# Row attention of the middle stage in eight slots, with TensorE in program order and the masked queries on ScalarE

## The chip, the cores and the metric

The kernel runs on one core of a Trainium2 chip. The metric is device time in microseconds, the median of several executions. Such a core has five engines that run side by side and wait for each other by semaphores: TensorE (matrix products and transposing[...]), VectorE, ScalarE, GpSimd, and SyncE, which here only issues DMAs. PSUM has eight banks per partition; this kernel uses six of them under one tag (`mm`) and two under another (`sm`).

## The reference

The input x has shape (4, 64, 256, 256). Layer 0 is a restormer-like block: layer normalisation over channels, a gated attention branch, a convolutional feed-forward branch whose result passes an 8x8 patch FFT with a learned filter, and residual additions. Layer 1 is attention along rows, then along columns, then a small MLP. The change lies in the piece that ends layer 0 and does the row attention of layer 1. Cut to that:

```python
# end of layer 0: 1x1 product, 8x8 patch FFT filter, residual
y = _conv1x1(y, out_w)
p = y.reshape(b, c, Hh // P, P, Ww // P, P).transpose(0, 1, 2, 4, 3, 5)
p = jnp.fft.irfft2(jnp.fft.rfft2(p) * fW, s=(P, P))
x = x + p.transpose(0, 1, 2, 4, 3, 5).reshape(b, c, Hh, Ww)
# layer 1, along each row; H = 4 heads, one query and one key value per head
q = jax.nn.elu(x @ wq.T + bq) + 1.0
k = jax.nn.elu(x @ wk.T + bk) + 1.0
q = q / q.mean(axis=3, keepdims=True)
k = k / k.sum(axis=3, keepdims=True)
ktv = jnp.einsum('brhcd,brhce->brhde', k, v)
o = jnp.einsum('brhcd,brhde->brhce', q, ktv)
h = xe + o.swapaxes(2, 3).reshape(b_, r_, c_, e_) @ wo.T + bo   # x is _ln(xe)
```

## The kernel before

The program runs in stages, each with its own pools: a, b and c1 (attention and input side of layer 0), c2 (depthwise convolutions as banded products), c3 (this change), d (column attention and MLP). c2 leaves its result in DRAM (`yd`), c3 leaves the hidden state in DRAM (`hd`), and d reads it.

Stage c3 works on tiles `(pr, s)`: a pair of images and a strip of eight image rows, 64 tiles in all. Per tile there are five generators, each a part of the work:

- `product` (line 962): the 1x1 product. For each of four row pairs r, two matrix products (line 970), one per image of the pair, with 512 columns; ScalarE copies the result to `zc` (line 971). Then 16 transposing products in groups of four (line 980), copied to `zs` by ScalarE (line 981).
- `patches` (line 985): for each half, the DFT of the patches (line 997), VectorE's multiplication with the filter into `fs` (line 1001), the inverse (line 1007), the residual addition into `xe` (line 1010), and the layer norm's sums (lines 1013 to 1018); at the end ScalarE's square root (line 1021) and VectorE's reciprocal into `rs`.
- `features` (line 1026): four times, `xe` is transposed (line 1033), copied to `xrT` by ScalarE (line 1035) and multiplied with the query and key weights into the `sm` bank `qk` (line 1038, "score"). Then VectorE transposes the result (line 1043), scales it and adds a bias, ScalarE takes the exponential (line 696), VectorE forms `f` (line 1050) and `kr` (line 1056). `f` is spread into masked copies for each of eight image rows: keys `kx` by eight ScalarE activations (line 1058), queries `qx` by one GpSimd multiplication (line 1059). Row sums go into `qj` and `kj` on VectorE (lines 1065, 1066).
- `attend` (line 1069): sums of keys times `xe` (line 1079), two products for the row sums (lines 1081, 1082), eight transposing products of `qx` (line 1095) with ScalarE's copies, a folding product (line 1100), and `mix` (line 699, product at line 702), which ends in `bdm` (line 1106).
- `update` (line 1109): four products of one row for the bias (line 1115), eight products of `qT` with `bdm` (line 1119), four VectorE additions into `h1` (line 1121), four DMAs issued by GpSimd (line 1125).

The loop at line 1131 runs n from 0 to 67. It first issues the loads of tile n + 1 from SyncE (`ya` and `xmp`), then gives `_steps` (line 241) five generators for five different tiles: `product` of tile n, `patches` of n - 1, `features` of n - 2, `attend` of n - 3, `update` of n - 4. `_steps` asks each in turn for its next part up to a `yield`, round after round, until all are exhausted. In 60 of the 68 loops all five are present.

The order in which the generators speak is the order of the program. It isn't yet the order on the engines: a planner places the instructions of each engine with its own model of costs and readiness, and within one engine may put a later instruction ahead of an earlier one. Stage d switches that off for TensorE:

```python
with tc.manual_schedule(engines={mybir.EngineType.PE}):
```

Inside it, TensorE's instructions stand in the order of the program, while the other engines are still placed by the planner. Stage c3 has no such line. The engines themselves take what they were given in order: an instruction that waits holds up those behind it on its engine.

Buffers that bear on this: `zc`, `fs`, `qTr`, `u`, `f`, `h1` have one buffer, `xe` and `xmp` three, most others two.

Of the kernel before, what the change touches and what calls it, by code (L numbers as in the profile page):

```python
# [9 lines left out]
F32 = mybir.dt.float32  # L10
AF = mybir.ActivationFunctionType
ALU = mybir.AluOpType
# [237 lines left out]
def kernel(ctx: ExitStack, tc: tile.TileContext, x, packs, fd, out, off):  # L250
# [670 lines left out]
    def stage_c3():  # L921
        NS = H // 8
        with ExitStack() as cs:
# [38 lines left out]
            def product(pr, s):  # L962

                ya, _ = ld[pr, s]

                zc = p.tile([128, 32, 32, 2], F32, name="zc", bufs=1)
                for r in range(4):
                    t = mm()
                    for b in (0, 1):
                        T.matmul(t[b * 64:(b + 1) * 64, :], owT, ya[:, :, 2 * r:2 * r + 2, b * 64:(b + 1) * 64].rearrange("p f y t -> p y f t"), start=True, stop=True)  # L970
                    S.copy(zc[:, :, 8 * r:8 * r + 8].rearrange("p j f t -> p f j t"), t.rearrange("p (f j t) -> p f j t", f=8, t=2))
                    if r % 2:
                        yield
                zs = p.tile([128, 16, 2 * C], F32, name="zs")
                zss[pr, s] = zs
                for k in range(4):
                    t = mm()
                    for i in range(4):
                        j = 2 * (4 * k + i)
                        T.transpose(t[:, i * 128:(i + 1) * 128], zc[:, j:j + 2].rearrange("p j f t -> p (j f t)"), ident)  # L980
                    S.copy(zs[:, 4 * k:4 * k + 4].rearrange("p g c -> p (g c)"), t)
                    if k % 2:
                        yield

            def patches(pr, s):

                _, xmp = ld.pop((pr, s))
                zs = zss.pop((pr, s))
                xe = p.tile([128, 16, 2 * C], F32, name="xe", bufs=3)
                sv = p.tile([128, 32], F32, name="sv")  # L990
                for hf in (0, 1):

                    zh = zs[:, 8 * hf:8 * hf + 8].rearrange("p (n g) c -> p n (g c)", n=2)
                    ts = [mm(), mm()]
                    for pt in (0, 1):
                        for n in (0, 1):
                            T.matmul(ts[pt][n * 64:(n + 1) * 64, :], dfw[pt * 64:(pt + 1) * 64, :], zh[pt * 64:(pt + 1) * 64, n], start=True, stop=True)
                    fs = []
                    for pt in (0, 1):
                        f_ = p.tile([128, 512], F32, tag=f"fs{pt}", name=f"fs{pt}", bufs=1)  # L1000
                        V.tensor_tensor(f_.rearrange("p (g c) -> p g c", c=C), ts[pt].rearrange("p (g c) -> p g c", c=C), mid_bc(fw, 8), ALU.mult)
                        fs.append(f_)
                    yield
                    ts = [mm(), mm()]
                    for pt in (0, 1):
                        for n in (0, 1):
                            T.matmul(ts[n][pt * 64:(pt + 1) * 64, :], dfi[n * 64:(n + 1) * 64, :], fs[pt][n * 64:(n + 1) * 64, :], start=True, stop=True)
                    for n in (0, 1):
                        r = slice(8 * hf + 4 * n, 8 * hf + 4 * n + 4)
                        V.tensor_tensor(xe[:, r].rearrange("p g c -> p (g c)"), ts[n], xmp[:, r].rearrange("p g c -> p (g c)"), ALU.add)  # L1010
                    src = xe[:, 8 * hf:8 * hf + 8].rearrange("p g (b c) -> p (g b) c", b=2)
                    s1 = p.tile([128, 16], F32, name="s1")
                    V.tensor_reduce(s1, src, AX.X, ALU.add)
                    xc = p.tile([128, 16, C], F32, name="xc")
                    V.scalar_tensor_tensor(xc, bc(s1, C), -LN_S, src, ALU.mult, ALU.add)
                    sq = p.tile([128, 16, C], F32, name="sq")
                    S.activation(sq, xc, AF.Square)
                    V.tensor_reduce(sv[:, 16 * hf:16 * hf + 16], sq, AX.X, ALU.add)
                    yield
                sd = p.tile([128, 32], F32, name="sd")  # L1020
                S.activation(sd, sv, AF.Sqrt, bias=eps_t, scale=LN_S)
                rs = p.tile([128, 32], F32, name="rs")
                V.reciprocal(rs, sd)
                xes[pr, s] = xe, rs

            def features(pr, s):

                xe, rs = xes[pr, s]
                qk = sm()
                for k in range(4):  # L1030
                    t = mm()
                    for i in range(4):
                        T.transpose(t[:, i * 128:(i + 1) * 128], xe[:, 4 * k + i], ident)
                    xT = p.tile([128, 512], F32, name="xrT")
                    S.copy(xT, t)

                    for g in range(4):
                        T.matmul(qk[g * 32:(g + 1) * 32, k * 128:(k + 1) * 128], rw, xT.rearrange("p (j n) -> p j n", j=4)[:, :, g * 32:(g + 1) * 32],
                                 start=True, stop=True)
                    yield  # L1040

                qp = p.tile([128, 16, 32], F32, name="qp")
                V.transpose(qp.rearrange("p j m -> p (j m)"), qk)
# [12 lines left out]
                V.tensor_tensor(kr, f[:, :, 4:8], bc(rs, 4), ALU.mult)  # L1056
                for y in range(8):
                    S.activation(kx[:, :, y], kr, AF.Identity, scale=rmask[:, y:y + 1])
                G.tensor_tensor(qx, f[:, :, 0:4].unsqueeze(2).to_broadcast([128, 32, 8, 4]), mk.to_broadcast([128, 32, 8, 4]), ALU.mult)
                fr = p.tile([128, 2, 8], F32, name="fr")  # L1060
                V.tensor_reduce(fr, f.rearrange("p (j b) h -> p b h j", b=2), AX.X, ALU.add)
                qj = p.tile([128, 2, 2, 8, 4], F32, name="qj")
# [6 lines left out]
            def attend(pr, s):  # L1069

                xe, _ = xes.pop((pr, s))
                qx, kx, qj, kj = fes.pop((pr, s))
                yield
                zp = sm()

                for j in range(16):
                    for b in (0, 1):
                        g = (2 * b + j % 2) * 32
                        T.matmul(zp[g:g + 32, :64], kx[:, 2 * j + b].rearrange("p y h -> p (y h)"), xe[:, j, b * 64:(b + 1) * 64], start=(j < 2), stop=(j >= 14))
                qs = mm()  # L1080
                T.matmul(qs[:, 0:1], qj.rearrange("p d b y h -> p (d b y h)"), K0("ones"), start=True, stop=True)
                T.matmul(qs[:, 1:2], kj.rearrange("p b d y h -> p (b d y h)"), K0("ones"), start=True, stop=True)
                rz = p.tile([128, 1], F32, name="rz")
                V.reciprocal(rz, qs[:, 1:2])
                qr = p.tile([128, 1], F32, name="qr_")
                V.tensor_copy(qr, qs[:, 0:1])
                zn = p.tile([128, 65], F32, name="zn")
                G.memset(zn[:, 64:65], 0.5)
                V.tensor_scalar(zn[:, 0:64], zp[:, 0:64], rz, None, ALU.mult)
                qT = p.tile([128, 1024], F32, name="qTr", bufs=1)  # L1090
                for k in (0, 1):
                    t = mm()
                    for i in range(4):
                        j = 8 * k + 2 * i
                        T.transpose(t[:, i * 128:(i + 1) * 128], qx[:, 2 * j:2 * j + 4].rearrange("p a y h -> p (a y h)"), ident)
                    S.copy(qT[:, k * 512:(k + 1) * 512], t)
                yield
                t = mm()

                T.matmul(t[:65, :64], zn, K("rfold"), start=True, stop=True)  # L1100
                zT = p.tile([65, 2, 64], F32, name="zT")
                V.tensor_copy(zT, mid_bc(t[:65, :64], 2))
                yield
                m = mix(p, zT.rearrange("p j y -> p (j y)"), rgt, qr)
                bdm = p.tile([128, 4, 64], F32, name="bdm")
                V.tensor_tensor(bdm, mid_bc(m, 4), bc(K("jmask"), 64), ALU.mult)
                bds[pr, s] = xe, qT, bdm

            def update(pr, s):

                xe, qT, bdm = bds.pop((pr, s))
                h1 = p.tile([128, 2, 16, C], F32, name="h1", bufs=1)
                ts = [mm() for k in range(4)]
# [9 lines left out]
                for b in (0, 1):  # L1123
                    for a in (0, 1):
                        G.dma_start(hd[2 * pr + b, 8 * s:8 * s + 8, 8 * a:8 * a + 8], h1[a * 64:(a + 1) * 64, b])
                yield

            seq = [(pr, s) for pr in range(B // 2) for s in range(NS)]
            load(*seq[0])

            for n in range(len(seq) + 4):
                if n + 1 < len(seq):
                    load(*seq[n + 1])
                _steps(*(f(*seq[n - d]) for d, f in ((1, patches), (4, update), (3, attend), (2, features), (0, product)) if 0 <= n - d < len(seq)))

    stage_c3()

# [275 lines left out]
```

## Time and profile before

| | us |
|---|---|
| median of 3 runs | 8800.12 (8797.13 to 8805.94) |
| the profiled execution | 8803.6 |
| its span, first to last instruction | 8801.8 |
| stage c3, first product to last update on TensorE | 5056.8 to 6675 |
| stage d, first product | 6689.7 |

The page gives TensorE 93% of the span busy, VectorE 67%, ScalarE 52%, GpSimd 14%. In its rows a shape such as `128*64 128x512` means: a tile of the array with 128 rows and 64 columns, and a moving operand of 128 partitions by 512 elements. One fp32 product of the program is two matrix instructions in the trace. "TensorE" is PE in the rows, "VectorE" DVE, "ScalarE" ACT, "GpSimd" POOL. What stands in brackets after a row of the timeline is the idle time of the engine before it, and what ended it. Matrix instructions overlap in their pipeline, so the cost of a block is read from its start to the start of the next.

### The profile page before, as it was taken

What the parts mean: (1) busy time and instruction counts of PE and PEld (TensorE: products, weight loads), DVE (VectorE), ACT (ScalarE), POOL (GpSimd) and SP (SyncE); (2) the same over time, 40 slices, a digit from 0 to 9 for tenths busy, and PEclk for the clock granted to TensorE, in tenths of its full rate; (3) what the DMA queues carried; (4) which work ended last, traced back from release to release, by engine and by line L of the source; (5) the groups of instructions that cost most, each with busy time, mean ns of one, the idle gap of its engine ahead of it and who ended that gap; (6) DMA issues with size and microseconds to landing.
All of it is one profiled execution on the core that took longest, in us unless ns stands there. A gap on an engine that the chain in (4) does not pass through costs nothing. (4 is left out here: it accounts for less than half of the span.)

```text
span 8801.8 us, 143151 instructions
## 1 busy us (share of the span) xinstructions
PE 8178.1 (93%) x57518; PEld 4216.6 (48%) x57518; DVE 5927.4 (67%) x8506; ACT 4601.7 (52%) x7779; POOL 1205.2 (14%) x1828
## 2 busy tenths in 40 slices
PE   8999999699999998999999999999997999999998
PEld 6777777344444443333333344444443444444443
DVE  7766666377777774222222288888886888888886
ACT  4455455455555553222222266666663777777776
POOL 1111111212222221000000011111110010101011
PEclk9999999699999999999999999999997999999999
DMA  7777777799999998888888755555552232323232
GB/s 161 161 188 187 182 182 180 193 347 388 396 391 388 386 387 320 298 296 298 296 297 298 273 184 172 173 168 167 169 158 63 59 77 58 77 58 77 58 77 39
DMA packets 1258502, 1832.48 MB, mean 208 GB/s; under 512 B 335600, under 2 KB 1040112, under 8 KB 1196656
## 3 DMA queue, kind: packets, MB, share of 16 engines
q1 hardware_dynamic: 1053296, 1034.63, 39.0%
q0 software_dynamic: 204544, 788.69, 28.0%
q8 instruction: 456, 7.47, 0.3%
q14 instruction: 206, 1.69, 0.1%
HBM read 967.65 MB, written 788.53 MB: 200 GB/s over the span
## 5 line engine op out<-in xcount | busy, mean ns | idle before, releaser
L915 DVE TENSOR_TENSOR y<-ge,mm 128x512 f32<-128x512 f32 (+1 forms) x640 | 406.3, 635 | 1212.8 <-ACT ge L914 1212.8
L882 PE MATMUL mm<-t,w 128*128 128x512 f32 (+1 forms) x2560 | 1094.1, 566 | 18.8 <-DMA t<-td 18.8
L914 ACT ACTIVATE ge<-mm 128x512 f32<-128x512 f32 (+1 forms) x640 | 354.9, 555 | 1253.5 <-PE mm L889 1253.5
L775 PE MATMUL mm<-gp,wc 128*64 128x510 f32 (+1 forms) x3072 | 702.7, 596 | 90.8 <-DVE xm L785 51.4
L620 PEld LDWEIGHTS mm<-wqk,gp 128*128 128x128 f32 x6144 | 728.7, 197 | 99.2 <-issue 61.5
L882 PEld LDWEIGHTS mm<-t,w 128*128 128x128 f32 x2560 | 455.4, 190 | 647.5 <-issue 437.0
L620 PE MATMUL mm<-wqk,gp 128*128 128x128 f32 x6144 | 762.3, 282 | 1.1 <-POOL gp L589 0.9
L1341 PE MATMUL mm<-xfT,w 64*128 64x512 f32 x2048 | 620.9, 642 | 51.1 <-ACT hg L1343 26.8
L1343 ACT ACTIVATE hg<-mm,b 128x512 f32<-128x512 f32 x1024 | 634.1, 688 | 53.2 <-PE mm L1341 51.5
L830 ACT COPY tb<-mm 128x512 f32<-128x512 f32 x512 | 300.7, 588 | 632.4 <-PE mm L824 632.1
L889 PE MATMUL mm<-t,w 64*64 64x504 f32 (+1 forms) x5120 | 575.6, 555 | 0.0
L824 PE MATMUL mm<-xl,pack_c 64*128 64x512 f32 x2048 | 513.5, 601 | 8.1 <-ACT xl L812 4.7
L1358 PE MATMUL mm<-hg,pack_d 128*64 128x512 f32 x2048 | 505.8, 615 | 0.0
L775 PEld LDWEIGHTS mm<-gp,wc 128*64 128x64 f32 x3072 | 277.8, 137 | 470.5 <-issue 333.3
L316 ACT ACTIVATE ln_sq<-xn 128x1024 f32<-128x1024 f32 x256 | 274.3, 1072 | 365.4 <-DVE xn L314 365.3
L1365 POOL DMA_DIRECT2D out_dram<-st x128 | 209.1, 1638 | 1756.3 <-DVE fe L695 1543.6
L318 DVE TENSOR_REDUCE ln_v<-ln_sq 128x16 f32<-128x1024 f32 x256 | 312.0, 1219 | 186.0 <-ACT ln_sq L316 186.0
L970 PE MATMUL mm<-ya,pack_e 128*64 128x512 f32 x1024 | 381.2, 616 | 11.2 <-DMA ya<-yd 11.2
L828 DVE COPY tb<-mm 128x512 f32<-128x512 f32 x512 | 345.0, 685 | 24.0 <-PE mm L824 18.5
L1359 DVE TENSOR_SCALAR st<-mm,pack_d 128x512 f32<-128x512 f32 x256 | 281.1, 1098 | 117.9 <-PE mm L1358 117.6
L1341 PEld LDWEIGHTS mm<-xfT,w 64*128 64x128 f32 x2048 | 225.1, 192 | 276.1 <-issue 125.7
L1185 ACT ACTIVATE ln_sq<-xc 128x1024 f32<-128x1024 f32 x256 | 273.0, 1067 | 132.1 <-DVE xc L1183 132.1
(458 smaller groups left out, 15283.8 us busy)
## 6 DMA issues: line engine op xcount, KB each, us to landing
t<-td SPq DMA_DIRECT2D x256, 1152.0 KB, 9.9
td<-tb POOLq DMA_DIRECT2D x144, 1024.0 KB, 15.6
td<-tb POOLq DMA_DIRECT2D x288, 512.0 KB, 13.9
yd<-y POOLq DMA_DIRECT2D x128, 1152.0 KB, 10.1
ya<-yd SPq DMA_DIRECT2D x192, 512.0 KB, 5.7
xs<-in_x_dram SPq DMA_DIRECT2D x128, 512.0 KB, 6.8
projd<-pj POOLq DMA_DIRECT2D x256, 256.0 KB, 6.0
gp<-projd SPq DMA_DIRECT2D x128, 512.0 KB, 9.5
```

What stands on the lines that cost most here:

```text
L620: T.matmul(qp[:, k * 128:(k + 1) * 128], gp[:, 2 * i + k // 2, at + dx:at + dx + 128], wqk[:, dx, :], start=(dx == 0), stop=(dx == 2))
L775: T.matmul(tv[i * 64:(i + 1) * 64, :, o], wc[2 * pr + i][:, dx, :], gps[i][:, 2 * r:2 * r + 2, i_], start=(dx == 1), stop=False, skip_grou ...
L824: T.matmul(t, inT[q, hf * 128:(hf + 1) * 128], xls[b // 2, s][q, :, 2 * y:2 * y + 2].rearrange("p f y t -> p f (y t)"), start=True, stop=True)
L828: V.tensor_copy(o, i_)
L882: T.matmul(t[:, :n], w[:, 0:128], x_[:, c, :], start=True, stop=False, skip_group_check=True)
L889: T.matmul(t[po:po + 64, :n].rearrange("p (n c) -> p n c", c=64)[:, :, o], w[q:q + 64, 128:192], x_[q:q + 64, c, i_], start=False, stop=Tr ...
L914: S.activation(ge[:, :n], ts[0][k][:, :n], AF.Gelu)
L915: V.tensor_tensor(y[:, c, :].rearrange("p n c -> p (n c)"), ge[:, :n], ts[1][k][:, :n], ALU.mult)
L970: T.matmul(t[b * 64:(b + 1) * 64, :], owT, ya[:, :, 2 * r:2 * r + 2, b * 64:(b + 1) * 64].rearrange("p f y t -> p y f t"), start=True, sto ...
L1341: T.matmul(t, w1[rh * 64:(rh + 1) * 64, k * 128:(k + 1) * 128], xT[rh * 64:(rh + 1) * 64], start=True, stop=True)
L1343: S.activation(g, t, AF.Gelu, bias=b1[:, k:k + 1])
L1358: T.matmul(y[rh * 64:(rh + 1) * 64, :], w2[:, k, :], hg[k * 2 + rh], start=False, stop=(k == 1), skip_group_check=True)
```

## The change

Three things change, all in stage c3.

1. The loop at line 1131 is put under `tc.manual_schedule(engines={mybir.EngineType.PE})`, and the generators speak in the order attend, product, features, patches, update.
2. The `yield`s are placed anew, so that a loop has eight rounds, here called slots 0 to 7. `features` transposes one group ahead: its scores come two slots (for the last, one slot) after the transposing. On TensorE the slots hold: 0, product row pair 0, transposing 0, DFT of the first half; 1, bias and update; 2, product row pair 1, score 0, transposing 1, inverse of the first half; 3, product row pairs 2 and 3; 4, key sums and row sums, score 1, transposing 2, DFT of the second half; 5, query transposing; 6, fold, half of the `zc` transposing, score 2, transposing 3, inverse of the second half; 7, mix, the other half of the `zc` transposing, score 3.
3. `qx` is made by eight ScalarE activations in place of the one GpSimd multiplication, and `xe` has four buffers.

```diff
@@ product
-                    if r % 2:
+                    if r == 0:
                         yield
+                        yield
+                    if r == 1:
+                        yield
+                yield
+                yield
+                yield
                 zs = p.tile([128, 16, 2 * C], F32, name="zs")
@@ patches
-                xe = p.tile([128, 16, 2 * C], F32, name="xe", bufs=3)
+                xe = p.tile([128, 16, 2 * C], F32, name="xe", bufs=4)
...
                         fs.append(f_)
+                    yield
                     yield
...
                     yield
+                    if hf == 0:
+                        yield
@@ features
-                for k in range(4):
+
+                def up(k):
                     t = mm()
                     for i in range(4):
                         T.transpose(t[:, i * 128:(i + 1) * 128], xe[:, 4 * k + i], ident)
                     xT = p.tile([128, 512], F32, name="xrT")
                     S.copy(xT, t)
+                    return xT
+
+                def score(k, xT):
 
                     for g in range(4):
                         T.matmul(qk[g * 32:(g + 1) * 32, k * 128:(k + 1) * 128], rw, xT.rearrange("p (j n) -> p j n", j=4)[:, :, g * 32:(g + 1) * 32],
                                  start=True, stop=True)
-                    yield
+
+                xT = up(0)
+                for k in range(3):
+                    yield
+                    yield
+                    score(k, xT)
+                    xT = up(k + 1)
+                yield
+                score(3, xT)
...
-                G.tensor_tensor(qx, f[:, :, 0:4].unsqueeze(2).to_broadcast([128, 32, 8, 4]), mk.to_broadcast([128, 32, 8, 4]), ALU.mult)
+                for y in range(8):
+                    S.activation(qx[:, :, y], f[:, :, 0:4], AF.Identity, scale=rmask[:, y:y + 1])
@@ attend
-                yield
+                for k in range(4):
+                    yield
                 zp = sm()
...
                 V.tensor_scalar(zn[:, 0:64], zp[:, 0:64], rz, None, ALU.mult)
+                yield
                 qT = p.tile([128, 1024], F32, name="qTr", bufs=1)
@@ update
+                yield
                 xe, qT, bdm = bds.pop((pr, s))
...
                         G.dma_start(hd[2 * pr + b, 8 * s:8 * s + 8, 8 * a:8 * a + 8], h1[a * 64:(a + 1) * 64, b])
-                yield
@@ the loop
-            for n in range(len(seq) + 4):
-                if n + 1 < len(seq):
-                    load(*seq[n + 1])
-                _steps(*(f(*seq[n - d]) for d, f in ((1, patches), (4, update), (3, attend), (2, features), (0, product)) if 0 <= n - d < len(seq)))
+            with tc.manual_schedule(engines={mybir.EngineType.PE}):
+                for n in range(len(seq) + 4):
+                    if n + 1 < len(seq):
+                        load(*seq[n + 1])
+                    _steps(*(f(*seq[n - d]) for d, f in ((3, attend), (0, product), (2, features), (1, patches), (4, update)) if 0 <= n - d < len(seq)))
```

## The prediction

> **What bounds the kernel now.** First the stretches of the two stages that matter, because the change touches one and the other is ordered in the way the first will be. The columns are busy microseconds of TensorE, its weight loads, VectorE, ScalarE and GpSimd, then granted clock, DMA share and GB/s.
>
> ```profile
> 5121.30:6588.50 1467.20, 1387.00 (x12756) 724.88 (x12752) 1255.49 (x2304) 912.64 (x1653) 252.49 (x354) 1.00 0.54 169
> 6900.00:8600.00 1700.00, 1572.17 (x9352) 711.87 (x9349) 1448.37 (x1798) 1281.23 (x1847) 179.03 (x135) 0.98 0.34 68
> ```
>
> The first is the steady part of the middle stage (c3). Its loop repeats every 24.85 us (5600.19 to 5625.04 below), so 1467.2 us are 59 loops; 60 of the 68 have all five generators at work. A loop costs TensorE 23.5 us, VectorE 21.3, ScalarE 15.5, GpSimd 4.3. TensorE bounds it and looks full. So next the timeline of TensorE over one loop: start, length, instructions of one kind, idle before.
>
> ```profile
> 5600.55 1.93 PE L970 MATMUL mm<-ya,pack_e 128*64 128x512 f32 x6
> 5602.41 1.09 PE L1007 MATMUL mm<-fs,pack_e 64*64 64x512 f32 x8
> 5604.20 1.10 PE L1079 MATMUL sm<-xe,kx 128*32 128x64 f32 x64 [0.70 <-ACT kx L1058]
> ...
> 5607.13 1.07 PE L970 MATMUL mm<-ya,pack_e 128*64 128x512 f32 x2
> 5608.14 0.42 PE L1038 MATMUL sm<-xrT,rw 128*32 128x128 f32 x8
> ...
> 5611.98 0.82 PE L980 MATMUL mm<-pack_k,zc 128*128 128x128 f32 x6
> 5612.87 0.42 PE L1038 MATMUL sm<-xrT,rw 128*32 128x128 f32 x8
> 5613.23 0.44 PE L980 MATMUL mm<-pack_k,zc 128*128 128x128 f32 x2
> 5613.60 1.09 PE L1007 MATMUL mm<-fs,pack_e 64*64 64x512 f32 x8
> ...
> 5619.51 3.72 PE L1119 MATMUL mm<-bdm,qTr 128*128 128x256 f32 x16
> ...
> 5623.60 1.07 PE L970 MATMUL mm<-ya,pack_e 128*64 128x512 f32 x2
> 5625.04 0.42 PE L1038 MATMUL sm<-xrT,rw 128*32 128x128 f32 x8 [0.36 <-ACT xrT L1035]
> ```
>
> Costs are taken from one block's start to the next one's. The product L970 is torn: two instructions cost 1.01 us (5607.13 to 5608.14) and the other six 1.86 (5600.55 to 5602.41), so a half of the product costs 2.87. During the fill of the same stage the same eight instructions stand together:
>
> ```profile
> 5066.47 1.94 PE L970 MATMUL mm<-ya,pack_e 128*64 128x512 f32 x8
> 5068.33 1.09 PE L1007 MATMUL mm<-fs,pack_e 64*64 64x512 f32 x8
> ```
>
> They cost 1.86. The two images' products (128 rows by 64 columns of the array, written to the lower and the upper 64 partitions) start a few ns apart and run beside each other when they are neighbours; a lone one takes as long as a pair. TensorE is therefore busy, but not at its best.
>
> **The change, part by part.** TensorE's order becomes the program's. Its blocks in one loop, priced by the rows above and those left out of the fence: slot 0 product row 0 (1.00), transposing (0.53), first DFT (1.02); slot 1 bias (1.07), update (3.65); slot 2 product (1.00), score (0.36), transposing (0.53), second DFT (1.02); slot 3 two product rows (1.86); slot 4 attention sums (1.03), their row sums (0.47), score (0.36), transposing (0.53), DFT (1.02); slot 5 query transposes (0.99); slot 6 fold (0.17), eight zc transposes (0.96), score, transposing, DFT (1.91); slot 7 mix (0.53), zc transposes (0.96), score (0.36). The sum is 21.3 us. Against 24.85 it removes 1.88 from the product (5.74 to 3.86); 1.42 of waits (0.77 for kx, 0.44 for xrT at 5625.04, 0.21 for bdm before L1119); and 0.6 because the zc transposes are no longer cut by a score (0.89 + 0.37 to 0.96, twice); it adds 0.36 where a transposing or update block is now followed by another array shape.
>
> The question is which waits come in. TensorE now holds everything behind a waiting product, so I compare the latencies measured before with the room that the slots leave on a TensorE that never waits:
> - Score 3 to the masked keys: before, 5616.84 (last score's end) to 5628.99 (kx's end one loop on, 5604.14 + 24.85) is 12.15 us, most of it VectorE's queue. Slots 0 to 3 are 12.04. Short by 0.1.
> - Mix to bdm: 4.85 (5614.62 to 5619.46); room 5.5. DFT to its inverse: 3.25 at its fastest; room 4.0 and more. Transposing to score: 1.33; room 3.0 to 7.3.
> - PSUM: six banks. At slot 3 the update's last three banks wait for VectorE's adds (0.64 each, behind the feature chain's tail); laid out by hand with VectorE's durations the third product row waits about 0.8.
> - ScalarE: kx and qx can stand as one block of 16 x 0.306 = 4.9 us (eight kx take 2.45). A copy of xrT that comes just behind it meets a room of 4.2: a wait up to 1.3, nothing if it comes first. I take 0.4.
>
> These sum to 1.3. Each is bounded below by nothing (they cover one another: a TensorE that waited once has given the others room). Above, the other stage is the nearest row: it has TensorE in program order already and leaves it idle 1 - 1572/1700 = 7.5%, which would make 21.3 / 0.925 = 23.1, or 1.8 of waits.
>
> The masked queries leave GpSimd (1.97) for eight ScalarE activations like kx's: 8 x 0.306 = 2.45. ScalarE goes from 15.5 to 17.9 of a loop; hidden unless a TensorE product stands behind them (above). They also free VectorE:
>
> ```profile
> 5601.87 1.97 POOL L1059 TENSOR_TENSOR qx<-f,pack_e 128x1024 f32<-128x1024 f32 x1
> 5602.19 1.74 DVE L1065 TENSOR_TENSOR kj<-fr,pack_e 128x64 f32<-128x64 f32 x1
> 5603.85 0.21 DVE L1066 TENSOR_TENSOR qj<-fr,pack_e 128x64 f32<-128x64 f32 x1
> 5603.99 0.21 DVE L1065 TENSOR_TENSOR kj<-fr,pack_e 128x64 f32<-128x64 f32 x1
> ```
>
> The first kj ends with GpSimd's multiplication and takes 1.74; the second, of the same shape, 0.21. So VectorE goes from 21.3 to 19.7. [...]
>
> At no cost: the fourth xe buffer (8 KB a partition; before, L1010 waits for nothing but TensorE); the four output DMAs of the update, which now issue from GpSimd in slot 1 (4 x 0.56 issue and 3.9 to land, with most of a loop before h1 is written again; behind them on GpSimd stands only the memset of zn, needed five slots later); the loads, at the loop's top as before (landing 5.5, used a loop later, DMA share 0.54 to about 0.6). Were that cover gone, a late load would cost its 5 us once per loop. Fill and drain (from 5056.8 to the first update at 5121, and after 6588) are chains of latencies with TensorE often idle: qx now adds 2.45 to a chain, kj takes 1.5 from it, four times each; I take 0, with 10 us either way.
>
> Loop: 21.3 + 1.3 = 22.65 rounded; 24.85 - 22.65 = 2.2, times 60 full loops = 132 us. The span of 8801.8 becomes 8669.8; with the 1.8 around it the profiled execution goes from 8803.6 to 8671.6. That execution stands 3.5 above the median of 8800.1, so the forecast is 8668.
>
> **The rivals.**
> - TensorE hardly waits (loop 21.3 to 22.0). For it: all rooms but one exceed the measured latencies. Against: VectorE at 19.7 leaves 1.6 of slack for every dependency. At 21.3: 3.5 x 60 = 212, hence 8588.
> - The gain is mostly given back (23.6 to 24.8). One form: product pairs don't run beside each other, 1.88 stays, loop 24.5, hence 8779. Against it stand the fill's rows. Another form is the clock:
>
> ```profile
> 6639.46 6.68 PE L1119 MATMUL mm<-bdm,qTr 128*128 128x256 f32 x16 [0.89 <-DVE bdm L1106]
> ```
>
> In the drain, after gaps, the update took 6.68 instead of 3.72 (granted clock 0.80 and 0.69 there). [...]
> - Slower than before: the feature chain. The loop is that chain plus slots 4 to 7 (9.3), so it passes 24.85 once score 3 to kx takes 15.55 instead of 12.15. It would if ScalarE's order put the eight qx ahead of kx (2.45) and a Square of 1.06 ahead of the exponential: 15.66. With a further 1 us of queue the loop is 25.8, +57 us, hence 8857. Against it: qx stands behind kx in the program, so an order by program place puts kx first.
>
> **How the numbers follow.** Likeliest (22.0 to 23.6): 0.56, its own range 8629 to 8725. Hardly waits: 0.14. Mostly given back: 0.13, a little of it within no change. Slower: 0.17, a little of it too. A measurement of this kernel tells about 0.2% (17 us) from no change. So faster 0.80, same 0.04, slower 0.16. The range for 8 in 10 cuts off the deepest tenth of the gain side and the slower case: 8595 (loop 21.4) to 8790 (loop 24.7).
>
> **What would show it.** In the profile after: L970 in groups of 4, 4 and 8 at 1.00, 1.00 and 1.86; the zc transposes in eights; kj at 0.21; a loop of 22 to 23.6; TensorE's waits on kx, xrT and PSUM releases together near 1.3 a loop. I am wrong if L1079 waits for kx by more than 2 us a loop, if scores wait behind the 16 masked copies each loop, or if the clock in the stage falls below 0.95.

## The result, and the profile after

The changed kernel takes **8633.58 us**, median of 4 runs (8627.66 to 8643.85), against 8798.62 for the kernel before on the same chip: a ratio of 0.9814, with an interval of 0.9802 to 0.9826. The forecast was 8668 with a range of 8595 to 8790. The profiled execution took 8643.85 us, its span 8642.1; before, it was 8803.6 and 8801.8.

First the steady stretch of the middle stage in the changed kernel. The columns are busy microseconds of TensorE, its weight loads, VectorE, ScalarE and GpSimd, then granted clock, DMA share and GB/s.

```profile
5140.00:6400.00 1260.00, 1223.33 (x12258) 669.24 (x12258) 1116.53 (x2209) 986.09 (x2044) 131.09 (x285) 1.00 0.65 190
```

Fifty-nine loops lie between the update at 5114.23 and the one at 6427.25, so a loop takes 22.25 us instead of 24.85. In one loop VectorE is now busy 19.7 us (1116.53 / 1260 x 22.25) and ScalarE 17.4; they were 21.3 and 15.5. The clock stays at 1.00.

Next the timeline of TensorE over one loop. Line numbers moved: the scores are now L1051 (before L1038), the DFTs L1003 and L1014, the key sums L1102 (L1079), the update L1145 (L1119).

```profile
5599.72 0.42 PE L1051 MATMUL sm<-xrT,rw 128*32 128x128 f32 x8
5600.07 1.08 PE L970 MATMUL mm<-ya,pack_e 128*64 128x512 f32 x4
5601.08 0.66 PE L1043 MATMUL mm<-pack_k,xe 128*128 128x128 f32 x4
5601.67 1.09 PE L1003 MATMUL mm<-zs,pack_e 64*64 64x512 f32 x8
5602.69 1.14 PE L1141 MATMUL mm<-pack_e,one 1*128 1x512 f32 x8
5603.76 3.72 PE L1145 MATMUL mm<-bdm,qTr 128*128 128x256 f32 x16
5607.41 1.08 PE L970 MATMUL mm<-ya,pack_e 128*64 128x512 f32 x4
...
5608.78 0.66 PE L1043 MATMUL mm<-pack_k,xe 128*128 128x128 f32 x4
...
5610.38 1.94 PE L970 MATMUL mm<-ya,pack_e 128*64 128x512 f32 x8
5612.25 1.10 PE L1102 MATMUL sm<-xe,kx 128*32 128x64 f32 x64
...
5613.52 0.36 PE L1105 MATMUL mm<-pack_k,kj 128*128 128x1 f32 x2
5614.53 0.43 PE L1051 MATMUL sm<-xrT,rw 128*32 128x128 f32 x8 [0.65 <-ACT xrT L1045]
...
5621.01 1.04 PE L986 MATMUL mm<-pack_k,zc 128*128 128x128 f32 x8
5621.98 0.43 PE L1051 MATMUL sm<-xrT,rw 128*32 128x128 f32 x8
```

The product stands in groups of four, four and eight instructions: 1.01, 1.01 and 1.87 us from start to start, 3.89 in all. The `zc` transposes stand in eights (0.97). There is one wait in a loop: score 1 has a gap of 0.65 us for its transposed input, which makes its start 0.71 us later than in the runs below where it waits for nothing. From 5599.72 to 5621.98 it is 22.26 us, 2.59 less than before; times 60 full loops that is 155 of the 160 us by which the span is shorter. The stage's first product also comes 4.9 us earlier (5051.86 against 5056.80), which the change did not bring: in the runs it lies anywhere between 5050 and 5066. The fill (first product to first update) is 3.4 shorter, and the rest gives 4 back.

The timeline of ScalarE in the same loop says why score 1 waits:

```profile
5608.74 0.99 ACT L1081 ACTIVATE qx<-f,pack_e 128x128 f32<-128x128 f32 x3 [1.27 <-DVE f L1071]
5609.63 2.43 ACT L1079 ACTIVATE kx<-kr,pack_e 128x128 f32<-128x128 f32 x8
5611.97 1.56 ACT L1081 ACTIVATE qx<-f,pack_e 128x128 f32<-128x128 f32 x5
5613.43 0.58 ACT L971 COPY zc<-mm 128x512 f32<-128x512 f32 x1
5613.90 0.57 ACT L1045 COPY xrT<-mm 128x512 f32<-128x512 f32 x1
```

The transposing that feeds this score (L1043, 5608.78) ended on TensorE at about 5609.4. Its copy to SBUF comes at 5613.90, behind sixteen masked copies and one of `zc`. ScalarE's order has three of the `qx` copies ahead of `kx`; even so `kx` ended at 5612.06, just before the key sums that read it (5612.25). On VectorE the `kj` product, which took 1.74 us under GpSimd's multiplication, now takes 0.21. The other rows are the update's additions (L1147), which free its PSUM banks, and `kr` between them:

```profile
5607.15 1.22 DVE L1147 TENSOR_TENSOR h<-mm,xe 128x512 f32<-128x512 f32 x2
...
5608.62 0.68 DVE L1147 TENSOR_TENSOR h<-mm,xe 128x512 f32<-128x512 f32 x1
5609.22 0.28 DVE L1077 TENSOR_TENSOR kr<-f,rs 128x128 f32<-128x128 f32 x1
...
5609.92 0.68 DVE L1147 TENSOR_TENSOR h<-mm,xe 128x512 f32<-128x512 f32 x1
5610.52 0.21 DVE L1087 TENSOR_TENSOR kj<-fr,pack_e 128x64 f32<-128x64 f32 x1
```

### The profile page after: what moved, and what is told of

The parts are those of the page before. It is cut to its first block, busy times and chain, and to the rows that moved or that the text cites. A ratio compares the mean times of both kernels' runs of the same rounds, so it can differ in the third digit from the quotient of the medians.

```text
span 8642.1 us, 143479 instructions
## 1 busy us (share of the span) xinstructions
PE 8062.2 (93%) x57518; PEld 4185.5 (48%) x57518; DVE 5829.0 (67%) x8506; ACT 4728.1 (55%) x8291; POOL 1078.3 (12%) x1764
## 4 chain that ended last, share of the span: by engine, by line
PE 60%; ACT 18%; DVE 16%; issue 4%; DMA 2%; SPq 0%; POOL 0%; ACTq 0%; DVEq 0%; POOLq 0%
PE mm L882 12%; PE mm L889 6%; PE mm L775 4%; PE mm L620 4%; PE mm L824 3%; PE mm L1145 3%; PE mm L1367 2%; ACT xl L812 2%; ACT ln_sq L316 2%; PE mm L1384 2%; ACT hg L1369 2%; DVE xn L314 2%; DVE ln_s L1207 2%; PE mm L1043 2%; DVE xc L1209 2%
## 5 line engine op out<-in xcount | busy, mean ns | idle before, releaser
L889 PEld LDWEIGHTS mm<-t,w 64*64 64x64 f32 x5120 | 158.1, 132 | 374.4 <-issue 374.4
```

The lines of the kernel that those rows point to most:

```text
L889: T.matmul(t[po:po + 64, :n].rearrange("p (n c) -> p n c", c=64)[:, :, o], w[q:q + 64, 128:192], x_[q:q + 64, c, i_], start=False, stop=Tr ...
```

## The experiments

The theory: the slots (which products are neighbours, and how far each stands behind its inputs) bring nearly all of the gain, because column halves run beside each other and TensorE stops waiting; `qx` on ScalarE matters because it shortens VectorE's queue; what is left is the wait for `xrT`. The rivals: program order on TensorE alone brings the gain, or the move of `qx` alone does.

### The parts alone

**qx on ScalarE alone**, in the kernel before:

```diff
-                G.tensor_tensor(qx, f[:, :, 0:4].unsqueeze(2).to_broadcast([128, 32, 8, 4]), mk.to_broadcast([128, 32, 8, 4]), ALU.mult)
+                for y in range(8):
+                    S.activation(qx[:, :, y], f[:, :, 0:4], AF.Identity, scale=rmask[:, y:y + 1])
```

> The kernel before with one part of the change alone: the masked queries are made by eight ScalarE activations. Theory (TensorE's order and its waits are the gain, VectorE's freed 1.5 us a loop are not on the path): kj falls to 0.21 us, the loop stays at 24.85 or grows by up to 1 us because the query transposes stand right behind the key sums and now wait for 16 activations; 8790 to 8860 us. Rival (the gain comes from VectorE being freed of GpSimd's multiplication): 1.53 us x 60 loops less, about 8710 us.

Measured: 8828.16 us, ratio 1.0031 (1.0020 to 1.0041). The loop is 25.39 us, the key sums wait 0.96 for `kx` (0.70 before), and the product is still torn into six and two. Relieving VectorE alone makes the kernel slower.

**Program order alone**, in the kernel before, with the slots of before:

```diff
-            for n in range(len(seq) + 4):
+            with tc.manual_schedule(engines={mybir.EngineType.PE}):
+                for n in range(len(seq) + 4):
...
```

> The kernel before with its loop put under program order for TensorE and nothing else: old yields, old order of the generators, queries on GpSimd. Theory: the product's pairs stand together (1.9 us a loop less), but each score follows its transposing at once and waits about 0.9 us for ScalarE's copy, four times a loop, so the loop is 24.3 to 25.5 us, 8760 to 8840 us. Rival (program order is what pays, the slots add little): loop about 22.5, 8650 us.

Measured: 9217.88 us, ratio 1.0473 (1.0457 to 1.0488). The expectation missed by far; the loop is 31.85 in the mean. The timelines of TensorE and ScalarE, and the windows (columns as above), of this kernel:

```profile
5706.60 0.65 PE L1038 MATMUL sm<-xrT,rw 128*32 128x128 f32 x8 [6.18 <-ACT xrT L1035]
5707.19 3.59 PE L970 MATMUL mm<-ya,pack_e 128*64 128x512 f32 x8
```

```profile
5703.64 2.45 ACT L1058 ACTIVATE kx<-kr,pack_e 128x128 f32<-128x128 f32 x8 [3.46 <-DVE kr L1056]
5705.98 0.57 ACT L1035 COPY xrT<-mm 128x512 f32<-128x512 f32 x1
```

```profile
5707.00:5711.00 4.00, 4.00 (x20) 0.98 (x16) 0.00 (x0) 0.77 (x2) 0.25 (x1) 0.56 0.76 234
5200.00:6300.00 1100.00, 811.50 (x7518) 425.35 (x7516) 728.55 (x1345) 539.58 (x965) 146.78 (x205) 0.89 0.43 133
```

The first score stands right behind its transposing; its copy stands behind `kx` on ScalarE, and `kx` behind VectorE's feature chain. So TensorE idles 6.18 us. Then the clock falls: the product takes 3.59 us at a granted clock of 0.56 where it took 1.94. The forecast charges nothing for the clock. For the changed kernel that was right: its one wait is 0.65 and its clock 1.00. With the old slots, where the wait is 6.18, the clock of the steady stage is 0.89.

**The change without program order** (the loop of the changed kernel, with its slots, taken out of `manual_schedule`):

```diff
-            with tc.manual_schedule(engines={mybir.EngineType.PE}):
-                for n in range(len(seq) + 4):
+            for n in range(len(seq) + 4):
...
```

> The changed kernel without the line that puts TensorE in program order: the new yields and the new order of the generators alone, the planner places TensorE. Theory A (the slots decide: with each product some slots behind its inputs the planner has no reason to leave the program's order, and its steady loop comes out the same): loop 22.26, 8620 to 8650 us. Theory B (the line decides; without it the planner tears pairs again): one to two tears a loop, 8690 to 8750 us.

Measured: 8627.78 us, ratio 0.9808 (0.9794 to 0.9823), the same as the change. TensorE's order in the steady loop is the same one, with the same wait of 0.65. So the slots do it: given these `yield`s the planner arrives at the order by itself.

**The fourth buffer of xe** taken back to three:

```diff
-                xe = p.tile([128, 16, 2 * C], F32, name="xe", bufs=4)
+                xe = p.tile([128, 16, 2 * C], F32, name="xe", bufs=3)
```

> The changed kernel with three buffers of xe instead of four. Theory (the fourth buffer costs and brings nothing: VectorE, in order, writes the next xe just behind the update's last addition, 5611.06 against 5610.60): time 8628 to 8644. Rival (the fourth buffer is what lets the tile's halves start in slot 2): the inverse's addition or its PSUM bank is waited for, loop 22.7 or more, time above 8660.

Measured: 8641.36 us, ratio 0.9825 (0.9809 to 0.9842), which can't be told from the change; the same single wait of 0.65. The fourth buffer brings nothing here.

### What the pairs are worth

The changed kernel, with the two halves of product row pairs 0 and 1 torn apart: the second image's half goes behind the transposing of the same slot.

```diff
-                    for b in (0, 1):
+                    def half(b, r=r, t=t):
                         T.matmul(t[b * 64:(b + 1) * 64, :], owT, ya[:, :, 2 * r:2 * r + 2, b * 64:(b + 1) * 64].rearrange("p f y t -> p y f t"), start=True, stop=True)
...
+                    half(0)
+                    if r < 2:
+                        late.append(other)
+                    else:
+                        other()
...
+                    _steps(*(gens.get(f) if f else rest() for f in (attend, product, features, None, patches, update)))
```

> The changed kernel with the two images' products of row pairs 0 and 1 torn apart: the second one is issued behind the scores and transposing of its slot, so that each stands alone. Same instructions, same work. Theory (neighbouring products run beside each other): each tear adds 1.0 us to TensorE's blocks, two a loop; the wait of 0.65 to 0.78 for a score may be covered by it, so the loop grows by 1.2 to 2.0 us, to 23.5 to 24.3 us, 8705 to 8755 us. Rival (the pairs' cost is the same either way and the gain came from fewer waits): loop within 0.3 us of 22.26, 8620 to 8650 us.

Measured: 8716.82 us, ratio 0.9905 (0.9890 to 0.9920), loop 23.53, TensorE busy without a gap. Four lone halves now stand in its timeline where two pairs stood, each as long as a pair:

```profile
5709.46 1.07 PE L979 MATMUL mm<-ya,pack_e 128*64 128x512 f32 x2
5711.05 1.07 PE L979 MATMUL mm<-ya,pack_e 128*64 128x512 f32 x2
...
5717.79 1.07 PE L979 MATMUL mm<-ya,pack_e 128*64 128x512 f32 x2
5719.73 1.07 PE L979 MATMUL mm<-ya,pack_e 128*64 128x512 f32 x2
```

Two tears cost 2.0 us; the wait for `xrT` (0.71) disappears behind them, which leaves 1.27 a loop. This confirms the 1.88 that the prediction took from the pairs.

### Where qx stands

**qx back on GpSimd**, in the changed kernel:

```diff
-                for y in range(8):
-                    S.activation(qx[:, :, y], f[:, :, 0:4], AF.Identity, scale=rmask[:, y:y + 1])
+                G.tensor_tensor(qx, f[:, :, 0:4].unsqueeze(2).to_broadcast([128, 32, 8, 4]), mk.to_broadcast([128, 32, 8, 4]), ALU.mult)
```

> The changed kernel with the masked queries back on GpSimd in one multiplication, all else as changed. Theory: the wait of score 1 for its copy (0.65 to 0.78 us a loop, behind kx and qx on ScalarE) goes, the first kj takes 1.7 us again; the loop is 21.5 to 22.3 us, 8590 to 8640 us. Rival (freeing VectorE is the gain): VectorE has 21.3 us of work again and holds the loop, 1.5 us x 60 more than changed, about 8725 us.

Measured: 8661.54 us, ratio 0.9840 (0.9826 to 0.9855), loop 22.72: slower than my expectation and far from the rival's. The wait for `xrT` is gone, but two others are there. The timelines of GpSimd, VectorE and TensorE:

```profile
5711.51 1.95 POOL L1080 TENSOR_TENSOR qx<-f,pack_e 128x1024 f32<-128x1024 f32 x1 [13.13 <-DVE f L1071]
5711.94 1.67 DVE L1077 TENSOR_TENSOR kr<-f,rs 128x128 f32<-128x128 f32 x1
...
5714.75 1.08 PE L970 MATMUL mm<-ya,pack_e 128*64 128x512 f32 x4 [0.57 <-DVE h L1146]
5716.14 1.10 PE L1101 MATMUL sm<-xe,kx 128*32 128x64 f32 x64 [0.31 <-ACT kx L1079]
```

While GpSimd multiplies, VectorE's `kr` takes 1.67 us; in the changed kernel it takes 0.28. Behind it everything of VectorE is late: the update's last addition, which frees the PSUM bank that the product wants, and `kx`. These are the bank wait and the `kx` wait that the prediction had put into the changed kernel. So `qx` on ScalarE is worth 0.46 us a loop (28 us) with the new slots, though it costs 28 us with the old ones. And the slots without it are 139 us faster than the kernel before on the same chip (8800.59), of the change's 165: they bring most of the gain.

**qx ahead of kx**, in the changed kernel:

```diff
                 for y in range(8):
-                    S.activation(kx[:, :, y], kr, AF.Identity, scale=rmask[:, y:y + 1])
-                for y in range(8):
                     S.activation(qx[:, :, y], f[:, :, 0:4], AF.Identity, scale=rmask[:, y:y + 1])
+                for y in range(8):
+                    S.activation(kx[:, :, y], kr, AF.Identity, scale=rmask[:, y:y + 1])
```

> The changed kernel with the eight qx activations ahead of the eight kx. On ScalarE all 16 then stand as a block with kx last, kx ends 5 x 0.306 = 1.5 us later. Theory (the feature chain closes the loop: score 3 to kx, then slots 4 to 7): chain 12.0 + 1.5 = 13.5, plus 9.4, loop 22.9; the wait moves from score 1 to the key sums and is 1.4 us there; 8660 to 8680 us. Rival (the chain has slack, ScalarE's total is what counts): unchanged, 8620 to 8650 us.

Measured: 8687.23 us, ratio 0.9875 (0.9860 to 0.9890). Loop and wait are close to what was expected, the time is 7 us over its upper end:

```profile
5715.35 1.10 PE L1102 MATMUL sm<-xe,kx 128*32 128x64 f32 x64 [1.25 <-ACT kx L1081]
```

The loop is 22.87. That is the slower rival's mechanism, switched on by hand: the loop follows the chain from score 3 to `kx`. In the changed kernel it stands 0.2 us short of deciding.

**Five of the eight qx copies later**, issued by `attend` in slot 3, where they come behind the `xrT` copy:

```diff
-                for y in range(8):
+                for y in range(3):
                     S.activation(qx[:, :, y], f[:, :, 0:4], AF.Identity, scale=rmask[:, y:y + 1])
...
                 for k in range(4):
+                    if k == 3:
+                        for y in range(3, 8):
+                            S.activation(qx[:, :, y], f[:, :, 0:4], AF.Identity, scale=rmask[:, y:y + 1])
                     yield
```

> The changed kernel with five of the eight qx activations issued by attend in slot 3, behind the copies of slot 2 in the program's order; three stay in features. ScalarE's copy for score 1 then stands ahead of these five. Theory: the wait before score 1 (0.74 us a loop) goes, the query transposes two slots later still find their qx; loop 21.5 to 21.7, 8588 to 8605 us. Rival (another wait takes its place, for instance the query transposes for the late qx, up to 1 us): 8625 to 8660 us.

Measured: 8606.14 us, ratio 0.9780 (0.9763 to 0.9796), loop 21.71, TensorE busy without a gap. The last wait of the loop is gone, and 27 us with it: it was the queue on ScalarE.

### A clock that falls while TensorE is busy

With patches ahead of features, a DFT stands between the key sums and the waiting score, and gives its copy 1 us more:

```diff
-                    _steps(*(f(*seq[n - d]) for d, f in ((3, attend), (0, product), (2, features), (1, patches), (4, update)) if 0 <= n - d < len(seq)))
+                    _steps(*(f(*seq[n - d]) for d, f in ((3, attend), (0, product), (1, patches), (2, features), (4, update)) if 0 <= n - d < len(seq)))
```

> The changed kernel with patches ahead of features in each slot, so that the DFT of slot 4 (1.02 us) stands before score 1. Theory (the 0.65 to 0.78 us before score 1 is the only wait left in a loop, and it is a copy behind kx and qx on ScalarE): score 1 comes 1.0 us later and no longer waits; the inverse of slot 6 comes 0.9 us earlier and may wait up to 0.5 for fs; loop 21.5 to 22.0, 8588 to 8620 us. Rival (VectorE at 19.7 us holds the loop through some other dependency): 8625 to 8650 us.

Measured: 8726.66 us, ratio 0.9919 (0.9904 to 0.9934). The wait was gone, and the kernel 93 us slower than the change. The timeline of TensorE and three windows of this kernel:

```profile
5712.07 1.09 PE L1003 MATMUL mm<-zs,pack_e 64*64 64x512 f32 x8
5713.09 0.66 PE L1043 MATMUL mm<-pack_k,xe 128*128 128x128 f32 x4
5713.68 2.17 PE L1141 MATMUL mm<-pack_e,one 1*128 1x512 f32 x8
5715.78 5.39 PE L1145 MATMUL mm<-bdm,qTr 128*128 128x256 f32 x16
```

```profile
5712.37:5715.78 3.41, 3.41 (x21) 1.02 (x13) 3.41 (x6) 3.10 (x4) 0.00 (x0) 1.00 0.55 216
5715.78:5719.20 3.42, 3.42 (x9) 2.79 (x9) 2.85 (x8) 2.49 (x5) 0.00 (x0) 0.50 0.04 14
5719.20:5722.61 3.41, 3.41 (x21) 1.79 (x20) 3.12 (x9) 2.94 (x11) 0.00 (x0) 1.00 0.00 0
```

Two things are worse. The bias (one partition by 512, four products in four strips of 32 partitions) takes 2.10 instead of 1.07: three products start together at 5713.68, the fourth at 5714.73, alone and as long as all four. Just before, at 5714.70, ScalarE ends the `xrT` copy that empties the transposing's PSUM bank. And the update takes 5.3 instead of 3.65: for 3.41 us TensorE has half its clock (0.50). Yet in the 3.41 us ahead of that it was busy all the time, with the DFT, the transposing and the bias. Every loop is like this: the loop is 23.90 us, and one such stretch in each makes a mean clock of 1 - 0.5 x 3.41 / 23.90 = 0.93, which is the granted clock from 5200 to 6300 us.

To find which slot it is, the two orders were mixed: `slot0_swap` has the new order in slot 0 alone, `rest_swap` in all slots but slot 0.

```diff
-                    _steps(*(f(*seq[n - d]) for d, f in ((3, attend), (0, product), (2, features), (1, patches), (4, update)) if 0 <= n - d < len(seq)))
+                    live = [(d, f(*seq[n - d])) for d, f in ((3, attend), (0, product), (2, features), (1, patches), (4, update)) if 0 <= n - d < len(seq)]
+                    r = 0
+                    while live:
+                        order = (3, 0, 1, 2, 4) if r == 0 else (3, 0, 2, 1, 4)
+                        live.sort(key=lambda x: order.index(x[0]))
+                        live = [x for x in live if next(x[1], _DONE) is not _DONE]
+                        r += 1
```

(In `rest_swap` the condition is `r > 0`.)

> The changed kernel, but in slot 0 alone the first DFT comes ahead of the transposing, so that the transposing stands next to the bias; slots 2, 4 and 6 as in the changed kernel. Theory A (the clock drops because transposing, the one-row bias and the end of the update stand together): the drop of 3.4 us at half clock comes in each loop as with all four slots turned round, loop 23.9, time 8715 to 8735. Theory B (the other slots bring it): clock 1.00 in the steady stage, loop 21.5 to 22.3 according to whether the score's wait for xrT stays, time 8590 to 8640.

Measured: 8788.62 us, ratio 0.9986 (0.9980 to 0.9993), granted clock 0.94 over the stage. That is the drop of theory A, though not in each loop (35 in 51), and a cost that it had not, which puts the time 54 us above its range: here the fourth bias product shows its wait, and the block takes 2.70 us.

```profile
5706.68 0.66 PE L1046 MATMUL mm<-pack_k,xe 128*128 128x128 f32 x4
5707.27 1.13 PE L1144 MATMUL mm<-pack_e,one 1*128 1x512 f32 x6
5708.92 1.12 PE L1144 MATMUL mm<-pack_e,one 1*128 1x512 f32 x2 [0.52 <-ACT xrT L1048]
5709.97 5.41 PE L1148 MATMUL mm<-bdm,qTr 128*128 128x256 f32 x16
```

The bias needs four PSUM banks of six. The transposing just ahead of it holds one until ScalarE has copied `xrT` out. With the DFT between them, the copy has 1 us more, and all four bias products start together.

> The changed kernel, but in slots 2, 4 and 6 patches speaks ahead of features, with slot 0 left in its order (transposing, then DFT, then bias). Theory A (what stands next to the bias decides on the clock): clock 1.00 in the steady stage, no wait, loop 21.5 to 21.7, time 8590 to 8610. Theory B (the drop comes from slots 2, 4 and 6): loop 23.9 with granted clock 0.93, time 8715 to 8735.

Measured: **8569.51 us**, ratio 0.9738 (0.9723 to 0.9752), below what either theory gave. The windows of this kernel:

```profile
5140.00:6380.00 1240.00, 1240.00 (x12662) 691.02 (x12661) 1155.48 (x2288) 1020.03 (x2112) 135.07 (x294) 1.00 0.67 196
```

The loop is 21.19 us, with no gap and the full clock. Against the change's 22.26 the wait of 0.71 is gone, and where other products became neighbours two transposings cost 0.50 in place of 0.59 and `mix` 0.43 in place of 0.54. This is the fastest kernel of the study.

Does the long bias bring the clock down, or the place of the transposing? In `bias_alone`, `rest_swap` has its fourth bias product in the strip of the first, which is meant to make it stand alone; nothing is moved and no bank is held longer.

```diff
-                    T.matmul(ts[k], one[k * 32:k * 32 + 1, :], K("rowbo8")[k * 32:k * 32 + 1, :], start=True, stop=False, skip_group_check=True)
+                    r0 = k % 3 * 32
+                    T.matmul(ts[k], one[r0:r0 + 1, :], K("rowbo8")[r0:r0 + 1, :], start=True, stop=False, skip_group_check=True)
```

> The kernel with patches ahead of features in slots 2, 4 and 6 only (8569.5), but the fourth bias product uses the strip of 32 partitions of the first, so that it can't run beside the other three; no product moves, no bank is held longer. The bias block goes from 1.07 to about 2.1 us a loop. Theory A (a stretch of 2 us in which one to three rows of the array are at work brings the clock down, as where the fourth product came late for want of a bank): half clock for 3.4 us in each loop, the update 5.3 instead of 3.65, loop 21.2 + 1.0 + 1.7 = 23.9, granted clock 0.93, time 8720 to 8740. Theory B (the transposing's place beside the bias brings it, whatever the bias takes): clock 1.00, loop 22.2, time 8625 to 8640.

Measured: 8639.14 us, ratio 0.9822 (0.9807 to 0.9837); loop 22.03, the bias 1.91 in place of 1.07. By the numbers that is theory B, but not cleanly: the granted clock is 0.98, not 1.00, for there are 11 half-clock stretches in 56 loops. The timeline and windows of one of them:

```profile
5223.73 0.66 PE L1046 MATMUL mm<-pack_k,xe 128*128 128x128 f32 x4
5224.31 1.09 PE L1006 MATMUL mm<-zs,pack_e 64*64 64x512 f32 x8
5225.33 1.98 PE L1145 MATMUL mm<-pack_e,one 1*128 1x512 f32 x8
5227.24 5.41 PE L1149 MATMUL mm<-bdm,qTr 128*128 128x256 f32 x16
```

```profile
5223.90:5227.31 3.41, 3.41 (x21) 1.20 (x20) 3.41 (x5) 3.39 (x4) 0.00 (x0) 1.00 0.98 355
5227.31:5230.72 3.41, 3.41 (x9) 2.77 (x9) 2.98 (x8) 2.37 (x6) 0.00 (x0) 0.50 0.11 46
```

Here DFT and transposing are in the good order, and the clock falls all the same, when 3.41 us are filled by transposing, DFT and bias. So neither theory as I had put it: it is not the order as such, and a long bias does not bring it in each loop. Nor does the length of the stretch from the product to the update decide alone. It is 2.68 us in the change, in `rest_swap` and in `qx_late`, where the clock stays at 1.00; 3.5 in `bias_alone`, with 11 drops in 56 loops; 3.7 in `patches_first`, with one in each of 52 loops; but 4.3 in `slot0_swap`, with 35 in 51. And `qx_ahead`, where it is 2.68 and the wait for `kx` 1.25, has two drops.

Set side by side, the granted clocks of the steady stage are these:

| kernel | the bias, us | longest wait of TensorE in a loop, us | granted clock |
|---|---|---|---|
| the change, `no_guard`, `xe3` | 1.07 | 0.65 | 1.00 |
| `rest_swap`, `qx_late`, `torn` | 1.07 | none | 1.00 |
| `qx_gpsimd` | 1.07 | 0.57 | 1.00 |
| `qx_ahead` | 1.07 | 1.25 | 1.00 |
| `guard_only` | 1.07 | 6.18 | 0.89 |
| `bias_alone` | 1.91 | none | 0.98 |
| `patches_first` | 2.10 | none | 0.93 |
| `slot0_swap` | 2.70 | 0.52 | 0.94 |

Busy time does not sort them: TensorE is busy without a gap in `patches_first` and in `rest_swap`, and the clocks are 0.93 and 1.00. With the new slots the mean clock was 0.98 or less in the three kernels whose bias takes 1.91 us or more, and `bias_alone` differs from `rest_swap` in the bias alone. Why some loops of `bias_alone` and `slot0_swap` have the drop and others not was not shown.

## Why the prediction was right, and where not

- **The sum without waits**, 21.3: measured 21.55 (22.26 less 0.71). A transposing costs 0.59 ahead of a DFT, not 0.53, four times. The pairs came as predicted (1.01, 1.01, 1.87), the `zc` transposes in eights at 0.97.
- **The waits**, 1.3 in three terms: measured 0.71 in one. The term for `kx` (0.1) is nothing: the chain is 11.99, not 12.15, and its room 12.18; what shortened it no run isolates. The term for the PSUM bank (0.8) is nothing and was the largest error: I had laid the update's additions behind the feature chain's tail, and on VectorE they stand between its steps (5607.15, 5608.62, 5609.92). The term for `xrT` (0.4, at most 1.3) is 0.71; its mechanism, a copy behind the masked copies on ScalarE, is confirmed by the run that moves five of them. That both missing waits appear with `qx` on GpSimd shows that they were near.
- **The signs of being wrong**: one of the three came. A score does wait behind the 16 masked copies in each loop. It marks a term that was too small, not another bound: 0.71 us where 0.4 was charged. The key sums wait for nothing, and the clock stays at 1.00.
- **Luck**: the sum was 0.25 too low and the waits 0.6 too high, so the loop is nearer to the forecast than its parts are.
- **The loop** was 22.65 and is 22.26; 0.39 x 60 = 23 us. The rest of the 34 us between forecast and median is the earlier first product (4.9), which is chance, the shorter fill (3.4, taken as 0), less the 4 given back later, and the profiled execution, which was 10 us above its median where I had taken 3.5.
- **qx on ScalarE**: VectorE 19.7 and `kj` 0.21 as predicted; ScalarE 17.4 for 17.9 (of a shorter loop). VectorE was not tried as its place; what is shown is that ScalarE's place beats GpSimd's by 28 us, with the new slots.
- **Program order**: all prices rested on TensorE's order, and the order came. The line that enforces it is not needed for it (`no_guard`).
- **The edits at no cost** held: the fourth buffer (three do as well), the output DMAs and the loads, none of which TensorE waits for.
- **The clock**: the forecast has no term for it, and it stayed at 1.00 with a wait of 0.65. It does not stay there in every kernel with TensorE in program order: with the old slots (`guard_only`) the longest wait is 6.18 us and the clock 0.89, and in a neighbour of this order (`patches_first`) it is 0.93 with no wait at all and a bias of 2.10 us, a length that the prediction had not looked at.
- **The slower rival** did not happen, but its chain is real: with `qx` ahead of `kx` the loop follows it. Its sum has a slip: a chain of 15.66 with 1 us more and 9.3 behind it is a loop of 25.96, not 25.8, hence 8867.

## What to carry to other kernels

When TensorE takes its products in order, place each of them by the queue of the engine that prepares its input, not by that engine's busy share: one copy behind sixteen others was the only wait left, and with the old places program order cost 7 us a loop. Keep products that use different strips or halves of the array next to each other, and see that all of them have their PSUM banks at that moment; here a lone half of the product took 1.07 us where the pair took 1.08, and a late bias product 1.05 where all four took 1.07. After reordering, read the granted clock beside the gaps: in `patches_first`, where the bias took 2.10 us, 3.41 us at half clock made the update 1.7 us longer in each loop although TensorE was never idle.

## What the runs showed of the hardware that I had not expected

- The half clock without a gap: 3.41 us long, in `patches_first` once in each loop of 23.90 us, with TensorE busy throughout (1100.00 of 1100 us).
- Four products of one row in four strips of the array take 1.07 us together (the change); one of them alone takes 1.05 (`slot0_swap`).
- GpSimd's multiplication (1.97 us in the kernel before, 1.95 with the new slots) stretches the VectorE multiplication that meets it: `kj` in the kernel before (1.74 for 0.21), `kr` with the new slots (1.67 for 0.28). With `kr` it lay on the path of the loop.
